# Three tiles' memberships as one stationary operand, a staged prologue, and the output written inside the loop of a graph-attention kernel

## Chip, core and metric

One NeuronCore of one Trainium2 chip runs the kernel; `num_devices=1`. The time is device microseconds (us) of one launch, the median of three runs. TensorE (PE, its weight loads PEld), VectorE (DVE), ScalarE (ACT), GpSimd (POOL) and SyncE (SP) each run their own instructions in order and wait for each other through semaphores. SP, ACT and POOL also issue DMAs.

## The reference, cut to what matters

A graph of 12,500 nodes and 412,500 edges, sorted by destination `dst`, is passed once through a four-head attention layer:

```python
h = jnp.maximum(_layernorm(x, axis=-1), 0.0)            # 12500 x 128
h = (h @ W_node.T).reshape(num_nodes, H, HD)            # H = 4, HD = 32
e = (edge_features @ W_edge.T).reshape(num_edges, H, HD)
att = jnp.sum(jnp.concatenate([h[src], h[tgt], e], -1) * a, -1)
att = jnp.where(att > 0, att, 0.2 * att)
m = jnp.maximum(segment_max(att, tgt), 0.0)
ex = jnp.exp(att - m[tgt])
denom = segment_sum(ex, tgt) + (num_edges - deg)[:, None] * jnp.exp(-m)
out = x + segment_sum((ex / denom[tgt])[:, :, None] * h[src], tgt)
```

So every edge needs one row of its source node, and rows are then summed over runs of edges with equal destination.

## The kernel before

**Prologue.** 12,500 nodes are 98 blocks of 128 (`NB`). Line 276 goes over groups of seven blocks: load `x` (SP), layer norm statistics (DVE, L289, L290), square root (ACT, L292), normalise and ReLU (ACT, L302), transpose (PE, L304; copied out by DVE, L306), project with the weights (PE, L309), copy out (ACT, L310), and store the group into a DRAM table of 140-float rows (`table`, L314, issued by ACT). A row holds the node's attention terms and its 128 projected values with a 1 after each head. Before this loop the kernel looks through the destinations: lowest destination and smallest step of each chunk of 896 edges (L207 to L217), from these the chunk's 32-wide window of nodes and several small rows (L224 to L262), and, for all edges at once, `key`, an edge's place in its chunk's window (L265 to L274, most of it on POOL). The whole prologue is ordered by a planner, not by the order of the code.

**Main loop.** A chunk is 7 tiles of 128 edges, a batch 8 chunks, and there are 461 chunks in 58 batches. This part is in `tc.manual_schedule()` (L560): each engine gets its instructions in the order of the code. For batch `b`:

* `gather` (L357): POOL issues one indirect DMA per tile (L364), which fetches 128 table rows into `hs`; 56 per batch, for batch `b+1` while batch `b` is worked on. Three small POOL copies, the gates (L360), stand ahead of the gathers of parts 0, 1 and 2 (18, 19 and 19 gathers, `STOPS`). A gate reads a result of earlier work, and so holds POOL until that work is done. Gate 0 reads the sums of batch `b-1` (`merged`), gate 1 the sums of the first two chunks of batch `b` (`s.pas`), gate 2 those of chunks 4 and 5.
* `weigh` (L398): when the 56 tiles of batch `b` have landed, DVE transposes the attention terms (`zst`, L402), and DVE and ACT find a running maximum per destination and the exponentials (`exr`).
* `scatter` (L429): for each chunk ACT and DVE make `rhs` (7 tiles x 140 columns; L442, L444), and PE multiplies it, tile by tile, with `hot`, the 128 x 32 membership of the tile's edges in the window (L449). Tile `i` goes to the 32 PE columns numbered `i % 4`. ACT copies the sums of two chunks out of PSUM (`keep`, L458).
* `begin` (L373): DVE makes `mem` (L377) and `hot` (L393), PE the attention terms `z` of batch `b+1` (L382, L385).
* `collect` (L462) adds the four column groups up on PE; every second batch `merge` (L475) rescales and scans 16 chunks on DVE (among it the two products of L514) and adds them to `acc` (L523), the sums of all nodes, in SBUF.
* After batch 3, `count_windows` (L525) counts chunks that do not fit one window.

**Rest.** `window()` (L621) handles those chunks in a loop on a count read from the chip. For these inputs the count is zero: the widest chunk spans 30 nodes. Then lines 802 to 833 turn `acc` into the output: weights, PE moves the heads back to rows, `x` is added, stores.

Of the kernel before, what the change touches and what calls it, by code (L numbers as in the profile page):

```python
# [11 lines left out]
I32 = mybir.dt.int32  # L12
# [22 lines left out]
COLS = NSC * CT  # L35
HALF = 4 * P
# [5 lines left out]
GB = 7  # L42
FH = 2 * H
# [12 lines left out]
def tiles_of(sc):  # L56

    return [T if c < NCH - 1 else max(LAST, 4) for c in (2 * sc, 2 * sc + 1) if c < NCH]


def filled(sc):

    return [T if c < NCH - 1 else LAST for c in (2 * sc, 2 * sc + 1) if c < NCH]

# [10 lines left out]
def kernel(  # L75
# [32 lines left out]
    key = const.tile([P, COLS], BF16, name="key")  # L108
    acc = const.tile([P, NQ, AW], F32, name="acc")
    nc.gpsimd.memset(acc, 0.0)  # L110
# [38 lines left out]
    def index(b):  # L149
        t = indices.tile([P, SB * CT], I32, name="src")  # L150
        nc.sync.dma_start(t, src[:, b * SB * CT:(b + 1) * SB * CT])
        return t

    early = [index(b) for b in range(2)]


    with (
        tc.tile_pool(name="prep1", bufs=1) as p1,
# [10 lines left out]
        dsts = p1.tile([P, COLS], I32, name="dsts")  # L169
        nc.scalar.dma_start(dsts, dst)  # L170
# [35 lines left out]
        for g in range(NG):  # L206
            n = min(P, NC2 - g * P)  # L207
            dch = p2.tile([P, CE], I32, name="dch")
            nc.sync.dma_start(dch[:n, :], dstc[g * P:g * P + n, :])
            nc.vector.tensor_reduce(ext[:n, g, 0:1], dch[:n, :], AX.X, OP.min)  # L210
            rise = p2.tile([P, CE - 1], I32, name="rise")
            nc.gpsimd.tensor_tensor(rise[:n, :], dch[:n, 1:], dch[:n, :CE - 1], op=OP.subtract)
            nc.vector.tensor_reduce(ext[:n, g, 1:2], rise[:n, :], AX.X, OP.min)
            pen = p2.tile([P, CE + 1], F32, name="pen")
            nc.gpsimd.memset(pen, -BIG)
            nc.vector.tensor_scalar(pen[:n, 1:CE], rise[:n, :], 0.0, -BIG, op0=OP.not_equal, op1=OP.mult)
            nc.sync.dma_start(pens[g * P:g * P + n, :], pen[:n, :])  # L217
        pb = [pps.tile([P, NC2], F32, name=f"pb{k}", bufs=1) for k in range(2)]
# [14 lines left out]

        floor = p1.tile([P, NC2], F32, name="floor")
# [24 lines left out]
        for a in range(4):  # L259
# [5 lines left out]
        dl = p1.tile([P, COLS], I32, name="dl")  # L265
        nc.vector.tensor_scalar(dl, dsts, W - 1, None, op0=OP.bitwise_and)
        rel = p1.tile([P, COLS], F32, name="rel")
        nc.gpsimd.tensor_copy(rel, dsts)
        nc.gpsimd.tensor_tensor(rel.rearrange("p (c t) -> p c t", t=T), rel.rearrange("p (c t) -> p c t", t=T),
                                floor[:, :, None].to_broadcast([P, NC2, T]), op=OP.subtract)  # L270
        nc.gpsimd.tensor_scalar(rel, rel, float(W), float(W), op0=OP.is_ge, op1=OP.mult)
        low_f = p1.tile([P, COLS], F32, name="dsts")
        nc.gpsimd.tensor_copy(low_f, dl)
        nc.gpsimd.tensor_tensor(key, rel, low_f, op=OP.add)  # L274

        for b0 in range(0, NB, GB):
            xg = p2.tile([P, GB, D], F32, name="xg")
            n = min(GB, -(-(N - b0 * P) // P))
            full = min(n, (N - b0 * P) // P)
            nc.sync.dma_start(xg[:, :full, :],  # L280
                              x[b0 * P:(b0 + full) * P, :].rearrange("(b p) d -> p b d", p=P))
            if full < n:
                nc.vector.memset(xg[:, full, :], 0.0)
                rest = N - (b0 + full) * P
                nc.sync.dma_start(xg[:rest, full, :], x[(b0 + full) * P:N, :])
            mv = p2.tile([P, GB, 2], F32, name="mv")
            for i in range(GB):
                stats = p2.tile([P, 6], F32, name="stats")
                nc.vector.bn_stats(stats, xg[:, i, :])  # L289
                nc.vector.bn_aggr(mv[:, i, :], stats)  # L290
# [138 lines left out]
    def scatter(s, follow):  # L429

        out = []
        for j in range(SB):
            sc = s.b * SB + j
            tiles = tiles_of(sc)
            if not tiles:
                continue
# [432 lines left out]
```

## Time and profile before

| what | us |
|---|---|
| median of three runs | 4327.94 (4326.93 to 4329.52) |
| profiled execution, its own time | 4340.74 |
| its span, first to last instruction | 4339.0 |
| start to first gather | 183.4 |
| first gather to end of the last | 4064.6 |
| end of the last gather to the end | 91.0 |
| POOL, DVE, PE, ACT busy | 3162.1, 1756.9, 1260.8, 453.5 |

The three stretches add up to the span. Busy time of an engine counts its instructions, not the time in which it waits or issues; a gather's issue between two gathers is therefore idle time of POOL in the page. PEclk is the share of TensorE's full clock that was granted, and was 0.595 on average.

### The profile page before, as it was taken

The page shows a single profiled execution, that of the slowest core. Times are in us where ns is not written, and L with a number is a line of the kernel's source. Part 1 is how long each engine was busy: PE and PEld are TensorE (multiplying, and loading weights), DVE is VectorE, ACT ScalarE, POOL GpSimd, SP SyncE. Part 2 cuts the span into 40 slices and gives each one's busy share as a digit, 9 for nine tenths or more (in the row PEclk, how much of TensorE's full clock was granted, in tenths as well). Part 3 has the DMA queues.
Part 4 walks back from the last instruction along what each step waited for, and adds up shares of the span by engine and source line. Part 5 has one row for each costly group of instructions (what it writes and reads, how often), then busy time and mean ns, then how long its engine had stood idle before and what let it go on. Part 6 is the DMA issues. An engine that isn't in the chain of part 4 may idle for free. (4 is left out here: it accounts for less than half of the span.)

```text
span 4339.0 us, 30729 instructions
## 1 busy us (share of the span) xinstructions
PE 1260.8 (29%) x9107; PEld 535.4 (12%) x9107; DVE 1756.9 (40%) x3136; ACT 453.5 (10%) x1430; POOL 3162.1 (73%) x3422
## 2 busy tenths in 40 slices
PE   3613131313232222313131323232232313131324
PEld 2301010101011110101010101111010101010101
DVE  7325343444334342534343433434253434343346
ACT  2301010100101010101010000101010101010010
POOL 5277777777777777777777777777777777777771
PEclk8556565656555655556565656565655656565655
DMA  3433433333343334343343434343434333343434
GB/s 96 139 91 94 112 106 93 105 91 109 86 110 85 109 86 109 86 108 103 93 106 89 110 87 110 85 110 86 109 85 109 96 99 104 90 108 88 109 86 129
DMA packets 235471, 434.48 MB, mean 100 GB/s; under 512 B 85642, under 2 KB 135814, under 8 KB 235174
## 3 DMA queue, kind: packets, MB, share of 16 engines
q0 software_dynamic: 103136, 231.23, 23.5%
q1 hardware_dynamic: 118678, 192.44, 13.5%
q10 hardware_dynamic: 13488, 8.82, 0.6%
q8 instruction: 73, 1.20, 0.1%
q14 instruction: 96, 0.79, 0.1%
HBM read 417.15 MB, written 15.09 MB: 100 GB/s over the span
## 5 line engine op out<-in xcount | busy, mean ns | idle before, releaser
L364 POOL DMA_INDIRECT hs<-table,src x3223 | 3072.6, 953 | 1067.5 <-issue 1043.4
L449 PE MATMUL pa<-rhs,hot 128*32 128x140 f32 x6448 | 516.8, 430 | 2900.8 <-DVE rhs L444 2888.2
L402 DVE STREAM_TRANSPOSE zst<-hs 128x224 f32<-128x224 f32 x58 | 23.9, 412 | 1867.0 <-DMA hs<-table,src 1867.0
L449 PEld LDWEIGHTS pa<-rhs,hot 128*32 128x32 f32 x6448 | 271.4, 152 | 3148.3 <-issue 2740.1
L444 DVE TENSOR_TENSOR rhs<-hs,exr 128x924 f32<-128x924 f32 x461 | 515.0, 1117 | 151.2 <-ACT rhs L442 151.2
L382 PE MATMUL z<-eft,wa 128*32 128x384 f32 (+1 forms) x928 | 433.2, 627 | 16.2 <-DMA twb<-table 16.2
L411 ACT ACTIVATE a<-z 32x224 f32<-32x224 f32 x232 | 80.5, 347 | 2057.6 <-DVE z L410 2057.6
L385 PE MATMUL z<-mem,twb 128*32 128x512 f32 x464 | 186.7, 546 | 3.9 <-DMA twb<-table 3.9
L382 PEld LDWEIGHTS z<-eft,wa 128*32 128x32 f32 x928 | 119.1, 128 | 305.9 <-issue 300.1
L442 ACT COPY rhs<-exr 128x28 f32<-128x28 f32 x461 | 97.9, 212 | 332.3 <-DVE rhs L444 276.9
L420 ACT ACTIVATE both<-a 32x224 f32<-32x224 f32 x232 | 89.9, 388 | 376.3 <-DVE a L417 372.0
L393 DVE TENSOR_TENSOR hot<-exr,key 128x448 f32<-128x448 f32 x231 | 127.5, 611 | 0.0
L523 DVE TENSOR_TENSOR acc<-acc,a 128x70 f32 x461 | 109.7, 238 | 34.3 <-DVE acc L523 19.6
L458 ACT COPY m<-pa 128x280 f32<-128x280 f32 x231 | 90.5, 392 | 310.9 <-PE pa L449 310.9
L410 DVE TENSOR_TENSOR z<-z,zst 32x224 f32<-32x224 f32 x232 | 89.8, 387 | 77.9 <-ACT a L411 71.9
L416 DVE TENSOR_TENSOR_SCAN m<-pen,up 32x896 f32<-32x896 f32 x58 | 116.4, 2008 | 7.8 <-DVE up L414 0.5
L414 DVE TENSOR_TENSOR_SCAN up<-pen,z 32x896 f32<-32x896 f32 x58 | 117.0, 2017 | 2.0
L485 DVE TENSOR_SCALAR mc<-r 128x16 f32<-128x16 f32 (+1 forms) x29 | 5.6, 192 | 249.1 <-ACT r L473 249.1
L377 DVE TENSOR_SCALAR mem<-mem,nid 128x896 f32<-128x896 int32 x116 | 81.2, 740 | 26.3 <-DMA mem<-in_dstc 26.3
L422 DVE SCALAR_TENSOR_TENSOR both<-pen,m 32x224 f32<-32x224 f32 x232 | 88.7, 382 | 2.4
L473 ACT COPY r<-t 128x280 f32<-128x280 f32 (+1 forms) x58 | 23.7, 409 | 592.3 <-PE z L385 591.4
L467 PE MATMUL t<-m,rsame 128*32 128x280 f32 (+1 forms) x464 | 73.4, 415 | 0.4 <-ACT m L458 0.4
(142 smaller groups left out, 994.9 us busy)
## 6 DMA issues: line engine op xcount, KB each, us to landing
eft<-in_ef SPq DMA_DIRECT2D x58, 1792.0 KB
mem<-in_dstc SPq DMA_DIRECT2D x116, 448.0 KB
hs<-table,src POOLq DMA_INDIRECT x3223
xg<-in_x SPq DMA_DIRECT2D x26, 448.0 KB
twb<-table SPq DMA_DIRECT2D x464, 0.5 KB
table<-rows ACTq DMA_DIRECT2D x14, 490.0 KB
pen<-pens SPq DMA_DIRECT2D x58, 112.1 KB
out<-o SPq DMA_DIRECT2D x13, 448.0 KB
```

Of the source, the lines that this page charges most:

```text
L364: nc.gpsimd.indirect_dma_start(out=s.hs[:, i, :], out_offset=None, in_=table[:, :], in_offset=bass.IndirectOffsetOnAxis(ap=s.src[:, i:i + ...
L382: nc.tensor.matmul(s.z[:, part], wa3[:, j, :], s.eft[:, j, part], start=(j == 0), stop=False)
L385: nc.tensor.matmul(s.z[:, part], twb[:, s.b % 2, k, :], s.mem[:, k, part], start=False, stop=(k == 1))
L393: nc.vector.tensor_tensor(hot, rows_ps[:, None, :].to_broadcast([P, CT, W]), key[:, sc * CT:(sc + 1) * CT, None].to_broadcast([P, CT, W]), ...
L414: nc.vector.tensor_tensor_scan(up, s.pen[:, :CE], s.z, 0.0, op0=OP.add, op1=OP.max)
L416: nc.vector.tensor_tensor_scan(m[:, ::-1], s.pen[:, CE:0:-1], up[:, ::-1], 0.0, op0=OP.add, op1=OP.max)
L420: nc.scalar.activation(both[g * R:(g + 1) * R, 0, :, :], grouped(att, g), AF.Exp)
L442: nc.scalar.copy(rhs[:, :n, :, HD + 2], s.mx[:, :n, q * H:(q + 1) * H])
L444: nc.vector.tensor_tensor(rhs[:, :n, :, :HB], s.hs[:, i0:i0 + n, FH:].rearrange("p t (h d) -> p t h d", h=H), s.ex[:, :n, q * H:(q + 1) * ...
L449: nc.tensor.matmul(pa[g * W:(g + 1) * W, c, :], s.hot[j][:, c * T + i, :], rhs[:, i, :, :].rearrange("p h k -> p (h k)"), start=(i < 4), s ...
L458: nc.scalar.copy(s.pas[:, 2 * j:2 * j + n, :], pa[:, :n, :])
L523: nc.vector.tensor_tensor(cols, cols, put[:, i0 + i, :, :], op=OP.add)
```

## The change

1. **`scatter`.** Three tiles' memberships stand side by side as one stationary operand of 96 columns, and three tiles' `rhs` as one moving operand of 420 columns. The result is 96 x 420, of which only the three 32 x 140 blocks on the diagonal mean anything. Seven tiles take three matmuls (tiles 0-2, tile 6 alone, tiles 3-5) instead of seven. `keep` is called for each chunk and copies the three blocks with three ACT copies; gate 1 reads the block sums of chunk 1 on 96 partitions. `collect` adds three groups.
2. **Prologue.** It is in manual order. Units of three blocks go through stages that are written out one after another (`measure`, `deviate`, `normalize`, `project`, `turn`, `keep_rows`), each unit a few rounds behind the next; `x` is loaded in groups of nine blocks, three loads ahead. The look through the destinations is spread over the rounds (`extents`), its loads go out on ACT's queue, and the chain of small rows stands after the last round. The clearing of `acc` comes after POOL's first two instructions on the destinations.
3. **`key`** is no longer made for all edges in the prologue, but per batch in `begin`, by four DVE operations on 128 x 56.
4. **`merge`** copies its 128 x 32 `lastm` part to PSUM (`here`) and multiplies from there.
5. **Output in the loop.** `parts()` says after which batch a run of blocks can no longer change. `finish` makes its output there, seven blocks at a time, in 15 parts; its store is issued in the next batch. `count_windows` also checks that this was allowed for the given input, and if not (or if there are windows) the loop at the end computes all output once more. For these inputs the check gives zero and the loop is not entered.

```diff
@@ tiles_of ... @@
+def parts():
+    got, b0 = [], 0
+    for n in [GB] * 13 + [3, NB - 13 * GB - 3]:
+        last = (b0 + n) * P + 2 * W
+        b = next((b for b in range(MB - 1, NBT, MB) if (b + 1) * CB * CE * N >= last * E), NBT - 1)
+        got.append((b0, n, b if b0 + n < NB else NBT - 1))
+        b0 += n
+    return got
@@ prologue @@
+        def extent(g):
+            rise = p2.tile([P, CE - 1], I32, name="rise", bufs=NG)
+            nc.gpsimd.tensor_tensor(rise[:n, :], dch[:n, 1:], dch[:n, :CE - 1], op=OP.subtract)
...
+            nc.vector.tensor_reduce(ext[:n, g, 0:1], dch[:n, :], AX.X, OP.min)
+            yield
+            nc.vector.tensor_reduce(ext[:n, g, 1:2], rise[:n, :], AX.X, OP.min)
+            yield
+            nc.vector.tensor_scalar(pen[:n, 1:CE], rise[:n, :], 0.0, -BIG, op0=OP.not_equal, op1=OP.mult)
+            nc.sync.dma_start(pens[g * P:g * P + n, :], pen[:n, :])
+            yield
...
+        while k < 0 or line:
+            u = next(units, None)
+            if u:
+                measure(u)
+            at = {j: v for j, v in line}
+            if k + 3 in at:
+                deviate(at[k + 3])
+            if k + 2 in at:
+                normalize(at[k + 2])
+            if k in at:
+                project(at[k])
+            if k + 2 in at:
+                turn(at[k + 2])
+            if k in at:
+                keep_rows(at[k])
...
+            if k > 6 and k % 2:
+                next(extents, None)
+            k += 1
+        for _ in extents:
+            pass
         pb = [pps.tile([P, NC2], F32, name=f"pb{k}", bufs=1) for k in range(2)]
...
-        nc.gpsimd.tensor_scalar(rel, rel, float(W), float(W), op0=OP.is_ge, op1=OP.mult)
-        low_f = p1.tile([P, COLS], F32, name="dsts")
-        nc.gpsimd.tensor_copy(low_f, dl)
-        nc.gpsimd.tensor_tensor(key, rel, low_f, op=OP.add)
@@ begin @@
+        nc.vector.tensor_scalar(dk, s.dst, W - 1, None, op0=OP.bitwise_and)
+        nc.vector.tensor_tensor(key.rearrange("p (c t) -> p c t", t=T), s.dst.rearrange("p (c t) -> p c t", t=T),
+                                floor[:, s.b * CB:(s.b + 1) * CB, None].to_broadcast([P, CB, T]), op=OP.subtract)
+        nc.vector.tensor_scalar(key, key, float(W), float(W), op0=OP.is_ge, op1=OP.mult)
+        nc.vector.tensor_tensor(key, key, dk, op=OP.add)
@@ scatter @@
-                for i in range(n):
-                    g = i % 4
-                    nc.tensor.matmul(pa[g * W:(g + 1) * W, c, :], s.hot[j][:, c * T + i, :],
-                                     rhs[:, i, :, :].rearrange("p h k -> p (h k)"),
-                                     start=(i < 4), stop=(i + 4 >= n), tile_position=(0, g * W))
-                if c == 0 and len(out) > 1:
-                    keep(s, *out[-2])
-                    follow(out[-2][0])
+                pa = ps.tile([P, G * H * AW], F32, name="pa", bufs=2)
+                order = [*range(0, n - G, G), n - G] if n % G == 0 else [0, n - n % G, *range(G, n - n % G, G)]
+                for i in order:
+                    w = min(G, n - i)
+                    nc.tensor.matmul(pa[:w * W, :w * H * AW],
+                                     s.hot[j][:, c * T + i:c * T + i + w, :].rearrange("p t r -> p (t r)"),
+                                     rhs[:, i:i + w, :, :].rearrange("p t h k -> p (t h k)"),
+                                     start=(i == order[0]), stop=(i == order[-1]))
+                if last is not None:
+                    keep(s, *last)
+                    if last[0] % 2:
+                        follow(last[0] // 2)
+                last = (q, pa)
+    def keep(s, q, pa):
+        for g in range(G):
+            rows = slice(g * W, (g + 1) * W)
+            nc.scalar.copy(s.pas[rows, q, :], pa[rows, g * H * AW:(g + 1) * H * AW])
@@ merge @@
-        here = lastm[:, c0:c0 + n, :]
+        here = ps.tile([P, MC, 2], F32, name="t2")[:, :n, :]
+        nc.vector.tensor_copy(here, lastm[:, c0:c0 + n, :])
@@ finish, new @@
+        nc.sync.dma_start(xg[:, :full, :], x[b0 * P:(b0 + full) * P, :].rearrange("(b p) d -> p b d", p=P))
...
+        nc.scalar.activation(em, acc[:, q, AW - 1], AF.Exp, scale=-1.0)
...
+        nc.vector.tensor_tensor(wgt[:, :n * 4, :], acc[:, q, :HD], em[:, :, None].to_broadcast([P, n * 4, HD]),
+                                op=OP.mult)
...
+        for h in range(H):
+            for s in range(4):
+                nc.tensor.matmul(po[s * W:(s + 1) * W, h // 2, h % 2, :n, :],
+                                 ident[:, h * W:(h + 1) * W], w4[:, :n, s, :], start=True, stop=True,
+                                 tile_position=(0, s * W))
+        for k in range(2):
+            cols = xg[:, :n, k * 2 * HD:(k + 1) * 2 * HD].rearrange("p b (h d) -> p h b d", d=HD)
+            nc.vector.tensor_tensor(cols, po[:, k, :, :n, :], cols, op=OP.add)
@@ main loop @@
+                for store in stores:
+                    store()
...
+            for b0, n, last in parts():
+                if last == b:
+                    stores.append(finish(work, ps, "up", em_ps, b0, n))
```

## The prediction, made before the changed kernel had run

> **What bounds the kernel now.** I read the page's costliest groups first, then the timeline at the start, through one late batch and at the end, and last the windows view for the granted clock.
>
> ```profile
> L364 POOL DMA_INDIRECT hs<-table,src x3223 | 3072.6, 953 | 1067.5 <-issue 1043.4
> ...
> L402 DVE STREAM_TRANSPOSE zst<-hs 128x224 f32<-128x224 f32 x58 | 23.9, 412 | 1867.0 <-DMA hs<-table,src 1867.0
> ```
>
> POOL's gathers are the bound: 953 ns busy and some 0.30 us of issue each. Their start-to-start interval is 1.252 us in the median; 3222 of these are 4034 us of the 4064.6 us between first and last gather. DVE meanwhile stands idle for 1867 us until a batch has landed. Only three things can move the end: when the first gather starts, what stretches gathers or holds a gate, and what follows the last one.
>
> ```profile
> 53.99 11.51 POOL L271 TENSOR_SCALAR rel<-rel 128x3248 f32<-128x3248 f32 x1
> 54.39 11.18 DVE L261 TENSOR_SCALAR nid<-top,rcol 32x116 f32<-32x116 f32 x1
> ...
> 183.43 1.18 POOL L364 DMA_INDIRECT hs<-table,src  x1 [110.43 <-issue]
> ```
>
> The start: until 76 us little of the node loop is done; POOL makes `key`, and a DVE instruction that elsewhere takes 0.31 us takes 11.18 beside it. Then eleven groups at 7.9 us each follow.
>
> ```profile
> 4209.10 0.20 POOL L360 COPY gate<-r 128x1 f32<-128x1 f32 x1
> ...
> 4210.85 0.41 DVE L402 STREAM_TRANSPOSE zst<-hs 128x224 f32<-128x224 f32 x1 [18.94 <-DMA hs<-table,src]
> ...
> 4223.86 1.12 DVE L444 TENSOR_TENSOR rhs<-hs,exr 128x924 f32<-128x924 f32 x1 [0.27 <-ACT rhs L442]
> ...
> 4225.13 1.15 PE L449 MATMUL pa<-rhs,hot 128*32 128x140 f32 x14 [49.03 <-DVE rhs L444]
> ...
> 4227.70 0.39 ACT L458 COPY m<-pa 128x280 f32<-128x280 f32 x1 [1.08 <-PE pa L449]
> ...
> 4231.70 0.19 POOL L360 COPY gate<-m 128x1 f32<-128x1 f32 x1
> ```
>
> One batch, with the end of its last gather as zero (4209.10): PE starts at 16.05, the first `keep` ends at 19.0, gate 1 runs at 22.6. So gate 1 has 3.6 us to spare; over all batches after the first it is 3.54 in the mean, and 0.13 in the batch after `count_windows`. This margin is what the change draws on.
>
> **The change part by part.**
>
> **(a) Prologue.** A unit is three blocks. DVE: statistics and their aggregation now wait for each other, one block 0.41 us (95.42 to 95.72 is one such wait, plus 0.11), three 1.23; reciprocal and shift 0.41, `hT` copy 0.53, ones and `tn` 0.2: 2.37. ACT: square root 0.30, three ReLUs 1.26 (row at 95.11), row copy 0.45: 2.0, and every third unit a DMA issue of 0.38 that waits for DVE's ones; I charge 0.19 per unit. PE at half clock: six projection passes 1.73 (76.54), three transposes 0.9: 2.63. Three engines nearly tie; I take 2.6. The destination steps add two reductions of 1.08 and one 0.62 for each of four groups, 9.5 within the rounds. First `x` at 7 us[...], POOL blocking DVE early 2, two short rounds 3, 31 x 2.6 = 80.6, 9.5, the last rounds 6: 108. Then the chain of small rows: in the built program the first gather waits for its last `nid`. The same instructions undisturbed are 12.6 us by their rows (`top` 1.12, fourteen of 0.62 to 0.64 or 0.38 to 0.46, `nid` 4 x 0.31), before them 2 for the last reduction and eight matmuls, after them 1 to POOL's start. Sum 124; with some rounds at the warm clock I take 122. Saved: 183.4 - 122 = **61**. Bounds: units of 2.37 give 115, units of 3.0 give 135: saved 48 to 70. The table's last store (landed 4 us after its issue) is covered by that chain.
>
> **(b) `key`.** Removed with (a). Four DVE operations per batch, 0.54 us together, lie in DVE's idle time. `mem` (L377), 1.4 us of a similar kind, stretched gathers by 0.1 us per batch; 0.54 us gives **+2**, bounds 0 to 8.
>
> **(c) `here` in PSUM.**
>
> ```profile
> 4180.80 2.12 DVE L514 TENSOR_TENSOR a<-up,lastm 128x544 f32<-128x544 f32 x2
> 4181.54 1.14 POOL L364 DMA_INDIRECT hs<-table,src  x1 [0.30 <-issue]
> ```
>
> Of the gathers that overlap L514, 26 are longer than 1.25 us, by 10.4 us in sum. L444, as long but with one operand in PSUM, stretches the gathers beside it hardly (114 intervals, 1.4 us in the gathers' own durations). The extra copy is 0.2 us per merge in DVE's idle time. **-9.5**, bounds -11 to -6.
>
> **(d) `scatter` and gate 1.** A chunk was 14 PE passes of 140 columns (each product is recorded as two) in four column groups that overlap: 1.15 us. Now it is four passes of 420 and two of 140, all through the same columns: 1960 streamed columns.
>
> ```profile
> 4237.90 0.18 PEld L382 LDWEIGHTS z<-eft,wa 128*32 128x32 f32 x1 [0.68 <-issue]
> 4238.75 0.18 PEld L382 LDWEIGHTS z<-eft,wa 128*32 128x32 f32 x1 [0.68 <-issue]
> ```
>
> ```profile
> 4225.00:4228.40 3.40, 2.79 (x38) 1.73 (x41) 2.40 (x3) 0.93 (x4) 2.49 (x4) 0.50 0.26 63
> ...
> 4236.00:4240.00 4.00, 4.00 (x11) 0.95 (x6) 2.15 (x4) 0.39 (x1) 3.08 (x4) 0.56 0.26 57
> 4240.00:4247.00 7.00, 7.00 (x27) 2.24 (x26) 0.00 (x0) 0.00 (x0) 5.26 (x6) 1.00 0.27 60
> ```
>
> The first two rows: passes of 512 columns stand 0.853 us apart at clock 0.50, so 1.67 ns a column, with their weight loads hidden. A chunk is then 3.27 us, two chunks 6.54. The Trainium skill (TensorE: Matmul & The Clock Gate, Part 3, Packing small matmuls) speaks against this edit: narrow outputs should be packed into distinct column groups, where it saw three run 2.38 times as fast. By its factor, spread over the old passes, the old chunk would be 14 x 0.233 / 2.38 = 1.37 us; the row has 1.15, which I use. Either way PE triples its time.
>
> The windows rows (PE's busy time first, PEclk third from the end) show the clock: 0.50 while PE was 82% busy in `scatter`, 1.00 only after a full stretch of `z`. The same page's Part 1 says that the clock doubles after one busy window of about 3.4 us that runs free of the program. By it, `scatter`, now without gaps, turns warm 3 to 6.3 us after its start, and two chunks take 4.8 to 6.4 us, 5.6 in the middle; by the old `scatter`'s row, 6.54. I follow the page, since `z` did turn warm within 4 us. So: 16.05 + 5.6, drain 0.15, three ACT copies (0.28 for a 140-column copy alone, 0.19 each behind another: 0.66), semaphores 0.1: 22.6, with ends 21.8 and 23.5. Gate 1 is due at 22.6. Spread evenly, the late part is 0.29 us in the mean, over 57 batches **+17**; bounds 0 and 57 x 0.95 = +54. Behind the gate stand 19 gathers, and behind these everything. Gates 0 and 2 have over 15 us. ACT's `rhs` copies now queue behind `keep`, which slows later chunks to some 2.3 us; the scatter ends about 7 us later, and DVE still had 18.9 us idle before `zst` in this merge batch.
>
> **(e) `count_windows`**, once: its batch had 0.13 us at gate 1; the later scatter and its 14 small fills make it late by about 7: **+7**, bounds 2 to 12.
>
> **(f) Output in the loop.** Removed at the end: from the last `acc` add (4281.9) to 4339. A part costs about 5 us of DVE and PE (weights 1.08, adds 4 x 0.32, PE 1.1 to 1.9, reciprocal 0.2, the rest small), 13 or 14 times, within the 18.9 us of idle DVE less 8 for (b) to (d). Without that cover it would be 70. Its loads and stores (448 KB, two per part on SP) come into a stage whose DMA share is 0.38; SP's next loads are due a batch later. **+1.5** for stretched gathers, bounds 0 to 10. After the last gather: PE's start 16.1; five chunks 5.6, then 2.3, 2.3, 1.4 give 27.7; `keep` and `collect` 1.7; the merge as before (4271.44 to 4281.87) and `here`, 10.6: 40. The last part is small (four blocks): exponential to adds 3.8, store issue 0.4, landing 2, leaving 1: 47. Before 91.0. **-44**, bounds -47 to -38.
>
> **Sum:** -61 + 2 - 9.5 + 17 + 7 + 1.5 - 44 = -87. The span 4339.0 becomes 4252. The profiled execution (4340.74) ran 12.8 above the median of the runs; taking 87 off that median gives **4241**.
>
> **The rivals.**
>
> *Gate 1 never feels the warm clock.* For: in the old `scatter` it mostly stayed at 0.50 until `z`. Against: PE had gaps then. +54 instead of +17: 4278.
>
> *Gate 1 holds nothing.* ACT's copies and the clock come out better and the prologue's units are 2.37: -17 and -7: 4217.
>
> *Slower: weight loads no longer hide.* The old products used four column groups; now each load goes to columns that are streaming. A 128-column load's record is 0.18 us at half clock, six per chunk, two chunks: +2.2 us on gate 1 at a cold clock, 3.1 late, 57 x 3.1 = 177 against 17: 4401. It turns the sign once gate 1 is late by (87 + 17) / 57 = 1.8 us per batch. Against it: `z` has all its loads in the same columns and stands exactly at its stream time.
>
> *It doesn't shorten the prologue*, since waits between stages add up to 3.4 us per unit: 4241 + 25 = 4266.
>
> **How the numbers follow.** Likeliest case 0.5 (4241, own range 4205 to 4265), cold gate 0.2, no hold 0.13, long prologue 0.07, slower 0.08, other 0.02. The range takes in the likeliest, the cold gate with the other upper bounds, and the no-hold case: 4198 to 4312. Within 0.2% (8.7 us, about what a measurement here can tell) 0.02; slower 0.09; faster 0.89.
>
> **What would show it.** First gather near 122 us; gathers beside L610 at 0.95; `pa` in three products, two chunks in 5 to 6.5 us, and the gate's row with a wait on ACT; after the last gather 47 us. Wrong if the first gather is after 140, if gate 1 waits over 1 us per batch, or if `zst` no longer waits for the DMA.

## The result, and the profile after

The changed kernel takes 4299.31 us (median of 4 runs, 4298.43 to 4300.09); the kernel before took 4328.73 us beside it. The ratio is 0.9932, interval 0.9914 to 0.9949: 29 us faster, where 87 were forecast. The time lies in the range that was given, far above its likeliest value.

The profiled execution took 4299.55 us, its span 4297.8. The span of before, 4339.0, was taken at a slightly slower pace of the gathers: their median interval was 1.252 us there and is 1.249 here, and 3222 x 0.003 = 9.7 us of the difference are that pace, not the change. This would also explain most of the 12.8 us by which the profiled execution of before stood above its median.

Costliest groups of the kernel after (busy us, mean ns of one, idle us before them and what ended most of it):

```profile
L447 POOL DMA_INDIRECT hs<-table,src x3223 | 3052.6, 947 | 1060.8 <-issue 1058.0
L539 PE MATMUL pa<-rhs,hot 128*96 128x420 f32 (+1 forms) x2762 | 1092.5, 519 | 2216.8 <-DVE rhs L531 2216.3
...
L493 DVE STREAM_TRANSPOSE zst<-hs 128x224 f32<-128x224 f32 x58 | 23.9, 411 | 1356.2 <-DMA hs<-table,src 1356.2
L553 ACT COPY m<-pa 32x140 f32<-32x140 f32 x1383 | 367.3, 266 | 762.8 <-PE pa L539 752.1
```

POOL's gathers are still the bound, and `zst` still waits for the last of them, so DVE kept cover (1356 us of it instead of 1867). New is what POOL itself waited for (us in total, times, longest):

```profile
POOL gate L443 <- ACT m L553: 63.4, 56, 5.5
```

Gate 1 holds in all 57 batches that have one (the trace puts a 57th wait, of 1.4 us, down to ACT's `rhs`). One batch in the timeline, to be read against the one shown of before:

```profile
2050.05 0.20 POOL L443 COPY gate<-r 128x1 f32<-128x1 f32 x1
...
2051.72 0.41 DVE L493 STREAM_TRANSPOSE zst<-hs 128x224 f32<-128x224 f32 x1 [8.59 <-DMA hs<-table,src]
...
2065.96 8.69 PE L539 MATMUL pa<-rhs,hot 128*96 128x420 f32 x18 [24.05 <-DVE rhs L531]
...
2067.57 0.18 PEld L539 LDWEIGHTS pa<-rhs,hot 128*32 128x32 f32 x2 [1.25 <-issue]
...
2072.75 0.82 ACT L553 COPY m<-pa 32x140 f32<-32x140 f32 x3 [1.71 <-PE pa L539]
...
2073.70 0.18 POOL L443 COPY gate<-m 96x1 f32<-96x1 f32 x1 [1.09 <-ACT m L553]
...
2074.38 0.97 POOL L447 DMA_INDIRECT hs<-table,src  x1 [0.51 <-issue]
```

With the end of the last gather (2050.05) as zero: PE starts at 15.9, the three copies of chunk 1 end at 23.5, the gate runs at 23.65 after a wait of 1.09, and the next gather needs 0.51 us of issue where it otherwise needs 0.30. Before, the gate ran at 22.6 and had 3.5 us to spare.

The start and the end of the kernel after:

```profile
62.03 0.48 ACT L315 COPY rows<-ph 128x420 f32<-128x420 f32 x1
...
65.16 0.49 ACT L315 COPY rows<-ph 128x420 f32<-128x420 f32 x1
...
67.22 0.51 ACT L315 COPY rows<-ph 128x420 f32<-128x420 f32 x1
...
110.53 1.29 DVE L395 TENSOR_SCALAR nid<-top,rcol 32x116 f32<-32x116 f32 x4
...
112.85 1.15 POOL L447 DMA_INDIRECT hs<-table,src  x1 [82.67 <-issue]
...
4245.94 0.39 DVE L501 TENSOR_TENSOR z<-z,zst 32x224 f32<-32x224 f32 x1 [2.83 <-PE z L468]
...
4260.15 8.92 PE L539 MATMUL pa<-rhs,hot 128*96 128x420 f32 x18 [13.78 <-DVE rhs L531]
...
4284.72 0.20 ACT L670 ACTIVATE exr<-acc 128x16 f32<-128x16 f32 x1 [8.74 <-DVE acc L619]
...
4289.78 1.24 SPq L694 DMA_DIRECT2D out<-xg  x1
```

The first gather starts at 112.85 (before 183.43), the last ends at 4240.88, and 56.9 us follow (before 90.9). So where the time went, span against span, with the intervals of the gathers sorted by their place in the batch:

| | forecast, us | measured, us |
|---|---|---|
| first gather (a) | -61 | -70.6 |
| gaps at gate 1 (d, e) | +24 | +82.3 |
| gaps at gates 0 and 2 | 0 | -0.8 |
| all other gaps, at equal pace (b, c, f in the loop) | -6 | -8.4 |
| after the last gather (f) | -44 | -34.0 |
| sum | -87 | -31.5 |

"Gaps" is the sum over all batches of start-to-start intervals less 1.252 us: 85.7 at gate 1's place after, 3.4 before. -31.5 and the pace of -9.7 make the -41.2 between the spans. One row carries the error: gate 1.

### The profile page after: what moved, and what is told of

It reads as the page before. It is cut to its first block, busy times and chain, and to the rows that moved or that the text cites. A ratio compares the mean times of both kernels' runs of the same rounds, so it can differ in the third digit from the quotient of the medians.

```text
span 4297.8 us, 25217 instructions
## 1 busy us (share of the span) xinstructions
PE 1767.8 (41%) x5421; PEld 572.8 (13%) x5421; DVE 1788.9 (42%) x3449; ACT 746.4 (17%) x2606; POOL 3107.8 (72%) x3417
## 3 DMA queue, kind: packets, MB, share of 16 engines
q0 software_dynamic: 103136, 231.23, 20.9%
## 4 chain that ended last, share of the span: by engine, by line
POOL 45%; issue 18%; DVE 14%; PE 9%; ACT 6%; DMA 5%; DVEq 0%; POOLq 0%; ACTq 0%
POOL hs L447 44%; PE pa L539 9%; DMA hs<-table,src 5%; DVE up L505 3%; DVE m L507 3%; ACT both L511 2%; DVE z L501 2%; ACT a L502 2%; DVE rhs L531 2%; DVE z L503 1%; DVE a L508 1%; DVE exr L517 1%; ACT m L553 1%; DVE zst L493 1%; POOL gate L443 0%
## 5 line engine op out<-in xcount | busy, mean ns | idle before, releaser
L539 PE MATMUL pa<-rhs,hot 128*96 128x420 f32 (+1 forms) x2762 | 1092.5, 519 | 2216.8 <-DVE rhs L531 2216.3
L539 PEld LDWEIGHTS pa<-rhs,hot 128*96 128x96 f32 (+1 forms) x2762 | 333.3, 159 | 2968.6 <-issue 2693.8
L553 ACT COPY m<-pa 32x140 f32<-32x140 f32 x1383 | 367.3, 266 | 762.8 <-PE pa L539 752.1
L465 PE MATMUL z<-eft,wa 128*32 128x384 f32 (+1 forms) x928 | 361.6, 543 | 23.3 <-DMA twb<-table 23.3
L465 PEld LDWEIGHTS z<-eft,wa 128*32 128x32 f32 x928 | 97.7, 110 | 283.0 <-issue 283.0
L684 PE MATMUL up<-a,ident 128*32 128x224 f32 (+2 forms) x480 | 45.2, 555 | 214.8 <-DVE a L677 214.8
L460 DVE TENSOR_SCALAR mem<-mem,nid 128x896 f32<-128x896 int32 x116 | 74.7, 685 | 21.9 <-issue 16.2
```

The lines of the kernel that those rows point to most:

```text
L465: nc.tensor.matmul(s.z[:, part], wa3[:, j, :], s.eft[:, j, part], start=(j == 0), stop=False)
L539: nc.tensor.matmul(pa[:w * W, :w * H * AW], s.hot[j][:, c * T + i:c * T + i + w, :].rearrange("p t r -> p (t r)"), rhs[:, i:i + w, :, :].r ...
L553: nc.scalar.copy(s.pas[rows, q, :], pa[rows, g * H * AW:(g + 1) * H * AW])
```

## The experiments

All are the kernel after with one edit, except where said. Ratios are to the kernel before on the same chip; the kernel after has 0.9932.

**1. Is it the scatter that holds gate 1?** Two ways: put the old `scatter`, `keep`, `collect` and gate back, or leave all as it is and let the gates stand four gathers later.

```diff
-                    nc.tensor.matmul(pa[:w * W, :w * H * AW], ...
+                    nc.tensor.matmul(pa[g * W:(g + 1) * W, c, :], s.hot[j][:, c * T + i, :],
+                                     rhs[:, i, :, :].rearrange("p h k -> p (h k)"),
+                                     start=(i < 4), stop=(i + 4 >= n), tile_position=(0, g * W))
...
-                        gather(batch(b + 1), 1 + j // 2, s.pas[:G * W, 2 * j + 1, 0:1])
+                        gather(batch(b + 1), 1 + j // 2, s.pas[:, 2 * j, 0:1])
```

> The kernel after with the scatter, keep, collect and gate read of before: 14 products of 32 x 140 in four column groups and one eviction per pair of chunks (part d alone undone; key, here in PSUM, output in the loop and the new prologue stay). Theory 1 (the growth of the loop is gate 1 waiting for the longer scatter): the wait at gate 1 falls from 63 us to about 0 to 5, gaps at the gate-1 position lose some 80 us, the loop from first to last gather is about 4045 us, and the tail falls by about 9 us with the shorter scatter: span about 4208, median about 4210. Rival (the loop grew because the added key, output parts and their DMAs stretch gathers or hold the gate): the loop stays at 4128 and the time stays at about 4290 to 4299. Rival 2 (the gate stands for something that will wait anyway elsewhere): less than 40 us gained.

```diff
-STOPS = (0, 18, 37)
+STOPS = (0, 22, 41)
```

> The kernel after with gates 1 and 2 standing four gathers later in the row (before gathers 22 and 41 instead of 18 and 37), nothing else. Gate 1 becomes due about 5 us later (4 x 1.25), some 27.6 us after the last gather, and its release comes at 23.6. Theory 1: it then holds nothing outside the batch after the window count (0 to 1 us there), the gap at that position loses 80 to 85 us, the tail stays at 57: about 4215 us. Rival (the wait moves to gate 2 or to the wait of zst): 4260 to 4299. The period of a batch falls from 71.65 to about 70.2 us and the starts of the scatter no longer stand at one phase of the clock's 3.413 us windows.

Measured: the old scatter 4220.14 us against 4337.84, ratio 0.973 (0.9713 to 0.9746); the later gates 4233.45, ratio 0.976 (0.9744 to 0.9776). What the gate waited for, old scatter first:

```profile
POOL gate L443 <- ACT rhs L533: 0.8, 1, 0.8
```

```profile
POOL gate L443 <- ACT m L553: 4.2, 1, 4.2
```

The gaps at gate 1 fell from 85.7 to 4.0 and 0.1 us, the loop from 4128.0 to 4057.6 and 4063.4 us, though both runs had the slower pace of 1.252 us, which accounts for the 10 us by which the old scatter missed its forecast of 4210. With the later gates the median batch takes 70.48 us. Only the one wait behind `count_windows` is left with the later gates. Both rivals fall: the key, the output parts and their DMAs don't carry the loss, and the wait doesn't come back elsewhere in full. A little does: gate 1's new place holds 7.4 us of gaps, 4.2 of them that one wait, and the loop is 5.8 us longer than with the old scatter. The old scatter also takes 8.5 us off the end (tail 48.4), as expected; the later gates leave it (57.6).

Then both gates were taken out, with the new scatter and with the old one. (The gates are no part of the result; gate 0 still keeps a batch's gathers behind the batch that read the same buffer.)

```diff
-STOPS = (0, 18, 37)
+STOPS = (0,)
...
-                    if b + 1 < NBT and j in (0, 2):
-                        gather(batch(b + 1), 1 + j // 2, s.pas[:G * W, 2 * j + 1, 0:1])
+                    pass
```

> The kernel after without gates 1 and 2: a batch's 56 gathers follow gate 0 in one row, nothing else is changed. Theory (the gates' only effect on the time is their wait and their own small cost): against the later gates (ratio 0.976 to before) it also loses the two gate copies and what stands around them, about 0.2 us a batch, 12 us: ratio about 0.973. Rival (without the gates the gathers run into something that the gates kept them from, a full queue or a buffer not free): the wait comes back at a gather or at gate 0, ratio 0.98 to 0.99.

> The kernel after with the scatter of before and without gates 1 and 2: a version meant to beat both kernels. From the run with the old scatter (ratio 0.973): its two gate positions and the ones behind them hold some 12 us above the median interval; without them the ratio is about 0.970. Rival: the gates cost nothing on the path, 0.973.

Measured: 4218.30 us, 0.9733 (0.9718 to 0.9748), and 4208.30 us, 0.971 (0.9696 to 0.9725), both against 4333.48. As expected, to 0.001. The last is the fastest version that was run: some 2.2% below the kernel after and 2.9% below the one before.

**2. Why did a chunk take longer than its streamed columns?** In the trace of after, chunk 0 takes 3.73 us at half clock, where 1960 columns at 1.67 ns make 3.27. The third product has a 32 wide stationary operand, the others 96. Taken with the 96 wide slice of its three tiles and written to the third diagonal block, it streams the same columns and never changes the width.

```diff
                     w = min(G, n - i)
-                    nc.tensor.matmul(pa[:w * W, :w * H * AW],
-                                     s.hot[j][:, c * T + i:c * T + i + w, :].rearrange("p t r -> p (t r)"),
+                    f = i if i == 0 or w == G else i + w - G
+                    nc.tensor.matmul(pa[:G * W, (i - f) * H * AW:(i - f + w) * H * AW],
+                                     s.hot[j][:, c * T + f:c * T + f + G, :].rearrange("p t r -> p (t r)"),
```

> The kernel after with the third product of a chunk (the single tile) taken with the same 96 wide stationary slice of its three tiles and written to the third diagonal block's columns: the same 140 streamed columns and the same kept result, but no change of the stationary operand's width inside a chunk. Theory 1 (the 0.46 us of a chunk above its stream time are weight loads that stand exposed where the width changes): chunk 0 takes 3.27 to 3.35 us instead of 3.73, and PE is through both chunks some 0.5 us earlier at the same clock phase. Rival (the exposure belongs to the start of a new accumulation or to new data, not to the width): chunk 0 stays at 3.7. For the time: linear theory 57 x 0.5 = -28, about 4270 us; lock theory: the scatter's start moves to about 0.3 us into the window, the period stays at 71.65 and the time at 4299, unless that phase lies too near the window's edge, and then the lock breaks and the time falls by 30 to 60 us.

Measured: chunk 0 of one batch, first in the kernel after, then in this run (both rows end 0.2 us behind the start of the next chunk, for they hold the modelled end of the last pass):

```profile
2065.96 3.94 PE L539 MATMUL pa<-rhs,hot 128*96 128x420 f32 x6 [24.05 <-DVE rhs L531]
```

```profile
2269.65 3.55 PE L540 MATMUL pa<-rhs,hot 128*96 128x420 f32 x6 [42.85 <-DVE rhs L531]
```

From start to start chunk 0 takes 3.34 us in nearly every batch (3.05 where the clock turned warm inside it), so 0.39 us of each cold chunk belonged to the change of width; the rival falls. The starts of the single passes in after say where: beyond its streamed columns a pass takes 0.13 us more ahead of the narrow product, 0.14 more behind it and 0.11 one pass later. The 0.08 us at the chunk's first pass stay with one width. The time is 4278.31 us against 4337.84, ratio 0.9864 (0.9848 to 0.9881), some 29 us below the kernel after. By time alone that is the plain sum of what was saved, the linear theory of the expectation. The scatter's starts tell more, and come next.

**3. Why is gate 1 late by nearly the same amount in every batch?** The forecast spread the warm clock's arrival evenly over 3 to 6.3 us after the scatter's start, as if the program and the clock's windows ran free of each other. (Every change of the granted clock in the trace falls on a grid of 3.413 us; a window is one step of it.) Three successive starts of PE's scatter in the kernel after:

```profile
2137.70 1.69 PE L539 MATMUL pa<-rhs,hot 128*96 128x420 f32 x2 [41.77 <-DVE rhs L531]
2209.29 1.69 PE L539 MATMUL pa<-rhs,hot 128*96 128x420 f32 x2 [41.65 <-DVE rhs L531]
2280.99 1.69 PE L539 MATMUL pa<-rhs,hot 128*96 128x420 f32 x2 [41.72 <-DVE rhs L531]
```

They are 71.59 and 71.70 us apart; the median over the run is 71.65, and 21 windows are 71.68. Put on the grid, most of the starts stand 1.05 to 1.4 us into a window, and after a disturbance they go back in steps (2.96, 2.13, 1.67, 1.47, 1.35, 1.27 us in six batches), while in the kernel before they are spread over the whole window. My second theory was that the batch period, from one start to the next, has locked to the clock: a scatter that starts later in its window meets the warm clock sooner after its start, and so is done less late; each microsecond of delay costs half a microsecond less at the gate, until 56 gathers and the wait make just 21 windows. Its rival is the plain sum.

The half can be read from the batches themselves. Behind that disturbance the starts stand 1.75, 0.92, 0.46, 0.26, 0.14 and 0.06 us beyond 1.21, about where they settle: each batch roughly halves the distance. The periods from these starts are 70.84, 71.22, 71.48, 71.56 and 71.61 us, shorter the later the start. A straight line through period against start (without the first six batches and those that a disturbance stretched) falls by 0.48 us for each us in after. It falls by 0.47 to 0.49 in the run with one width and in the next three below, taken over starts beyond 0.75 us; in the kernel before, where gate 1 has slack, it rises by 0.07. The two theories part further where a little is added or taken away.

```diff
             nc.scalar.copy(s.pas[rows, q, :], pa[rows, g * H * AW:(g + 1) * H * AW])
+            if q == 1 and g == 0:
+                nc.scalar.copy(s.pas[rows, q, :], pa[rows, 0:H * AW])
```

> The kernel after with one more copy of the first kept block of chunk 1, behind the same copy on ACT: about 0.27 us more before gate 1 in every batch, nothing else. Lock theory (the batch period has locked to 21 of the clock's windows, 71.68 us, because a later start of the scatter meets the warm clock earlier): the period stays at 71.65 us, the phase of the scatter's start moves by about twice the delay, from about 1.2 to about 1.75 us into the window, and the time stays within 8 us of 4299. Linear theory (what is added before gate 1 is added to the batch): 57 x 0.27 = +15, about 4315 us, period 71.92.

Measured: 4308.68 us against 4337.84, ratio 0.9932 (0.9916 to 0.9949), the same as without the added copy; the plain sum asked for 0.9968. The ratio alone proves little, since the pace of this run (1.252) lengthens the kernel before as well. Its starts:

```profile
2144.25 1.69 PE L539 MATMUL pa<-rhs,hot 128*96 128x420 f32 x2 [41.84 <-DVE rhs L531]
2215.86 1.69 PE L539 MATMUL pa<-rhs,hot 128*96 128x420 f32 x2 [41.77 <-DVE rhs L531]
2287.68 1.68 PE L539 MATMUL pa<-rhs,hot 128*96 128x420 f32 x2 [41.94 <-DVE rhs L531]
```

The median period is 71.69 us, and the starts have moved to about 2.2 us in the window. That is 1.0 us later than in after, not 0.55: this run's gathers had the slower pace (1.252), which adds 0.17 us to a batch, and the copy cost 0.30; twice their sum is 0.94. The 11th and the 49th start, in after and in this run:

```profile
919.12 0.98 PE L539 MATMUL pa<-rhs,hot 128*96 128x420 f32 x1 [24.06 <-DVE rhs L531]
...
3642.91 0.98 PE L539 MATMUL pa<-rhs,hot 128*96 128x420 f32 x1 [41.65 <-DVE rhs L531]
```

```profile
925.76 0.99 PE L539 MATMUL pa<-rhs,hot 128*96 128x420 f32 x1 [24.17 <-DVE rhs L531]
...
3649.59 0.98 PE L539 MATMUL pa<-rhs,hot 128*96 128x420 f32 x1 [41.85 <-DVE rhs L531]
```

The 38 batches between them take 2723.79 and 2723.83 us; 38 times 21 windows are 2723.84. By the plain sum pace and copy would have added 38 x 0.47 = 18 us. What was added came back as an earlier warm clock. The 9.4 us by which this run is longer than after (4308.68 for 4299.31) lie where the starts had not settled: 5.9 us in the first ten batches, while they move from 0.56 to 2.2 us in the window, and 3.2 in the last nine, which hold a disturbance.

The other side: the gate waits for fewer of the three kept blocks, so that it comes 0.27 or 0.54 us earlier.

```diff
-                        gather(batch(b + 1), 1 + j // 2, s.pas[:G * W, 2 * j + 1, 0:1])
+                        gather(batch(b + 1), 1 + j // 2, s.pas[:2 * W, 2 * j + 1, 0:1])
```

(and `s.pas[:W, ...]` for the second).

> The kernel after, with gate 1 (and 2) waiting for the first two of the three kept blocks only, 0.27 us less before the gate. Lock theory: the scatter's start about 0.55 us earlier in the window than in the kernel after at the same pace of gathers (1.05 at 1.252 us, 0.65 at 1.249), period 71.65 to 71.7, ratio 0.993. Linear theory: 57 x 0.27 = -15 us, ratio 0.9897.

> The kernel after, with gate 1 (and 2) waiting for the first kept block alone, 0.54 us less before the gate. Linear theory: 57 x 0.54 = -31 us, ratio 0.986. Lock theory: start 1.1 us earlier than in the kernel after: at 1.252 us a gather about 0.5, still inside, ratio 0.993; at 1.249 about 0.1, past the edge between 0.28 and 0.44, so that the lock breaks now and then and the ratio is 0.98 to 0.986.

Measured: 0.27 us less gives 4301.66 us against 4324.50, ratio 0.9947 (0.9933 to 0.9960), no gain; period 71.69. But this doesn't separate the theories: the gaps at gate 1 fell by 13.5 us, about what the plain sum says, and the intervals of one place in the batch, the 27th, grew by 16.2 (from 4.7 to 20.9). The 27th gather runs beside DVE's two `mem` products in `begin`; in after, and then in this run:

```profile
2298.97 1.28 DVE L460 TENSOR_SCALAR mem<-mem,nid 128x896 f32<-128x896 int32 x2
2299.43 1.05 POOL L447 DMA_INDIRECT hs<-table,src  x1 [0.30 <-issue]
```

```profile
2300.98 1.27 DVE L460 TENSOR_SCALAR mem<-mem,nid 128x896 f32<-128x896 int32 x2
2301.13 1.35 POOL L447 DMA_INDIRECT hs<-table,src  x1 [0.30 <-issue]
```

How long this gather takes goes with where it starts against the first product. In the median it starts 0.46 us behind it in after and takes 1.03 us; here 0.16 behind and 1.34; in the next run 0.11 ahead and 0.94, as most gathers do. So what the gate saved was spent again eight gathers later. The batch's own work did not change, and the starts stood at 1.33 us, not at the 0.65 expected.

0.54 us less gives 4265.03, ratio 0.9865 (0.9849 to 0.9880), which both theories allow. Its starts are no longer 71.68 apart:

```profile
2120.17 1.68 PE L539 MATMUL pa<-rhs,hot 128*96 128x420 f32 x2 [41.17 <-DVE rhs L531]
2191.43 1.69 PE L539 MATMUL pa<-rhs,hot 128*96 128x420 f32 x2 [41.14 <-DVE rhs L531]
2262.88 1.68 PE L539 MATMUL pa<-rhs,hot 128*96 128x420 f32 x2 [41.13 <-DVE rhs L531]
```

In the window they run 1.37, 1.45, 0.79, 0.43, 0.14 and then jump to 2.62, over and over: they slide towards the window's start, and where a scatter begins within 0.30 us of it (0.31 is already too late) the clock turns warm a whole window sooner, 3.1 us after the start instead of 6.5, the gate is early, and the next start jumps. The same saw-tooth shows in the run with one width, with its edge between 0.67 and 0.70 us. So the lock has an edge, and what a saving is worth depends on whether it reaches it.

A long delay, six copies instead of one:

> The kernel after with six more copies of the first kept block of chunk 1 on ACT: about 1.75 us more before gate 1 in every batch. Linear theory: 57 x 1.75 = +100 us against after (ratio to before about 1.016). Lock theory: a start one window length later gains at most 1.7 us, so no phase gives 21 windows any more; the starts move on by 0.5 to 2.2 us from batch to batch, most slowly at the window's edges, about 1.16 us in the mean: 57 x 1.16 = +66 us against after, ratio to before about 1.0085, and the phases are spread over the window again.

Measured: 4401.29 us against 4333.48, ratio 1.0159 (1.0143 to 1.0175): the linear theory's number, some 98 us more than after by the ratios, for 57 x 1.75 = 100, and my +66 is refuted. I had taken the edge at 0.7 us from the run with one width, where the scatter of after has it at about 0.3 (in this run 0.19 was early enough and 0.28 was not). The starts are not spread either: they alternate between about 0.5 and 2.65 us, and the periods between 73.8 and 72.9, which is 43 windows for two batches (146.8 us). So the time speaks for the sum, the phases for a lock to another ratio, and the time alone can't tell them apart here.

**4. Part (c) alone**, in the kernel before:

```diff
-        here = lastm[:, c0:c0 + n, :]
+        here = ps.tile([P, MC, 2], F32, name="t2")[:, :n, :]
+        nc.vector.tensor_copy(here, lastm[:, c0:c0 + n, :])
```

> The kernel before with one part of the change: in merge, the pairs of masks are copied to PSUM first and the products read them there (part c alone). Theory (the two long products slow the gathers beside them while both their operands lie in SBUF): the gathers beside them return to 0.95 us, loop and time -9.5 us (bounds -11 to -6), ratio 0.9978. Rival (the slowing is that of the output's or of any long DVE instruction): 0 us, ratio 1.000.

Measured: 4330.27 us against 4333.48, ratio 0.9991 (0.9982 to 1.0000), so -4 us within -8 and 0. In the trace the intervals at the four places where the products of `merge` lay lost 10.7 us (12.3 to 1.6), while some other places, at or just behind the gates, gained: all gaps together fell by 6.3 us at the run's own pace (1.251). The effect is there with the expected size, and part of it is given back.

**5. Runs on another chip.** The shorter gates were first run, beside the kernel after, on a chip where the kernel before took 5070 us.

> The kernel after once more, beside the two runs with a shorter gate, so that phases and intervals can be compared at the same pace of the gathers. Lock theory: at a median gather interval of 1.252 us (56 of them 0.17 us longer than at 1.249) the scatter's start stands at about 1.6 us in the window instead of 1.2, and the period is 71.65 to 71.7 us all the same; ratio 0.993. Linear theory: the period is longer by the gathers' 0.17 us, 71.82.

> The kernel after, with gate 1 (and 2) waiting for the first two of the three kept blocks of its chunk only: some 0.27 us less before the gate in every batch, nothing else. Lock theory: the scatter's start moves earlier in the window by about 0.55 us (to about 1.05 at the slow pace of gathers, 0.65 at the fast one), the warm clock comes that much later after it, the period stays at 71.65 to 71.7 and the ratio at 0.993. Linear theory: 57 x 0.27 = -15 us, ratio 0.9897.

> The kernel after, with gate 1 (and 2) waiting for the first kept block alone: 0.54 us less before the gate. Linear theory: 57 x 0.54 = -31 us, ratio 0.986. Lock theory: the phase would have to be 1.1 us earlier than in the kernel after. At the slow pace of gathers that is about 0.5 and still inside (the run with the long delay turned warm late down to 0.44): period and ratio unchanged, 0.993. At the fast pace it is about 0.1, past the edge: the window counts as busy from its start, the warm clock comes a window earlier, the lock breaks now and then, and the ratio is about 0.98.

> The kernel after once more, as the measure for the two runs with a shorter gate on the same chip. Ratio 0.993. Lock theory: the scatter's start at about 1.2 us in the window at a median gather interval of 1.249 us, 1.6 at 1.252, the period 71.65 to 71.7 either way.

> The kernel after, with gate 1 (and 2) waiting for the first two of the three kept blocks only, 0.27 us less before the gate. Lock theory: the start about 0.55 us earlier in the window than in the kernel after beside it (1.05 at the slow pace, 0.65 at the fast one), period 71.65 to 71.7, ratio 0.993 as there. Linear theory: 57 x 0.27 = -15 us, ratio 0.9897.

> The kernel after, with gate 1 (and 2) waiting for the first kept block alone, 0.54 us less before the gate. Linear theory: 57 x 0.54 = -31 us, ratio 0.986. Lock theory: start 1.1 us earlier than in the kernel after: at the slow pace about 0.5, still inside, ratio 0.993; at the fast pace about 0.1, past the edge between 0.28 and 0.44, so that the lock breaks now and then and the ratio is 0.98 to 0.986.

Measured, in two sets: the kernel after 5422.31 and 5416.27 us (1.0688 and 1.0686), 0.27 us less 5398.34 and 5402.76 (1.0649 and 1.0664), 0.54 us less 5347.42 and 5339.02 (1.0541 and 1.0537). The gathers had their usual length. The second run of the kernel after, ACT in one scatter, then what PE did meanwhile:

```profile
2121.74 0.21 ACT L529 COPY rhs<-exr 128x28 f32<-128x28 f32 x1
2136.30 0.82 ACT L553 COPY m<-pa 32x140 f32<-32x140 f32 x3 [14.35 <-issue]
2137.15 0.21 ACT L529 COPY rhs<-exr 128x28 f32<-128x28 f32 x1
2151.71 0.82 ACT L553 COPY m<-pa 32x140 f32<-32x140 f32 x3 [14.35 <-remote]
```

```profile
2121.12 4.28 PE L539 MATMUL pa<-rhs,hot 128*96 128x420 f32 x12 [0.29 <-issue]
2138.65 3.93 PE L539 MATMUL pa<-rhs,hot 128*96 128x420 f32 x6 [13.26 <-issue]
```

Two pauses of 14 us stand in this scatter. ACT is the engine that stands: PE had made the sums that it copies at 2136.30 by 2125.40, while DVE waits for ACT's next `rhs`, and PE for DVE. The trace names nothing of the program that ended them. Of the 47 waits of 13 to 15 us on ACT in the run 43 lie in every second batch. Here they stand between gates 1 and 2; over the run the gaps at gate 1 are 694 us and at gates 0 and 2 517. They swamp the phases, so these six runs say nothing on the lock. They do say that the change's sign isn't the same everywhere: there it made the kernel 6.9% slower, and the two kernels with a shorter gate lost a little less. Why this chip pauses, and why the change suffers more, stays open.

## Why the prediction was wrong where it was

**(d), the step that failed.** "Gate 1 is due at 22.6. Spread evenly, the late part is 0.29 us in the mean, over 57 batches +17; bounds 0 and 57 x 0.95 = +54." The mechanism was named rightly (longer scatter, gate 1, a wait on ACT) and the size was not: 1.13 us of wait in the mean and 0.2 us of slower restart behind it. (The forecast's own ends of 21.8 and 23.5 make the mean 0.24 us and the most 0.9; that slip is 3 us.) A gate that waits over 1 us per batch is also one of the signs of being wrong that the prediction named. Four terms were short:

- The chunks: 3.73 us each at half clock instead of 3.27, since the weight loads of `z`, which I took as the pattern, all have one width. Halved by the warm clock: 0.46 us at the end of chunk 1. The rival "weight loads no longer hide" had the right mechanism at 2.2 us for two chunks; it is 0.46 us per chunk, and experiment 2 shows that 0.39 of it sits at the change of width. (Its 0.18 us for a 128-column load are those of the full clock: the rows of L304 at 23 to 26 us in before, where the granted clock is 1.00. At half clock such a load takes 0.34 us there, L309, and a 96-column one 0.285 in after.)
- The clock: warm at about 5.6 us in nearly every batch, not evenly from 3 to 6.3. From the mean of 4.65, half of the difference is 0.45 us. The rule that I followed holds: the clock turns warm at the end of the first window that the scatter fills, but for at most its first 0.3 us. In these two rows of one scatter, PE's busy time stands first and the granted clock third from the end. That the arrival is spread evenly was my addition.

```profile
2065.90:2071.50 5.60, 5.54 (x10) 1.73 (x10) 1.54 (x2) 1.16 (x5) 4.24 (x5) 0.50 0.54 142
2071.50:2078.00 6.50, 6.05 (x19) 1.94 (x18) 2.93 (x3) 2.71 (x11) 3.98 (x5) 0.99 0.18 44
```

- ACT's three copies: 0.82 us, not 0.66. The 0.19 for a copy behind another was too low; each is 0.27.
- The semaphore, 0.13 for 0.1, and the restart of the gathers, 0.2, which was left out.

0.46 + 0.45 + 0.16 + 0.03 + 0.20 is 1.30 us on a gate that would have been due just then; 57 x 1.30 = 74 of the 82. The upper bound of +54 failed because it bounded only the clock and held every other term fixed. With the lock, though, the lateness isn't such a sum: the batch waits out what is missing to 21 windows (71.68 less the 70.3 that 56 gathers and the gates' own cost take, 1.38), as long as the terms together fall inside its reach. The added copy of experiment 3 shows this on one side. On the other side only the edge was seen, for the one saving that stayed inside it was spent again at the 27th gather.

**(a)** -70.6 for -61, just past the bound of -70. Row copies of three blocks follow each other in 2.06 us in the median, where I took 2.6 (the copies at 65.16 and 67.22 are such a pair; the step from 62.03 holds a reduction of the destinations). I had charged PE at half clock; it was granted 0.66 to 1.00 in the windows of this stage. The chain behind the rounds took 13 us as forecast, and the last `nid` is right ahead of the first gather.

**(c)**, **(b)** and the loop's part of **(f)**: -8.4 for -6, as forecast; (c) alone in the kernel before came out smaller in time than in its gathers. With the old scatter in place the added `key` and output parts leave the other gaps at 11.4 us, against 10.8 for (c) alone in the kernel before, at a pace 1 ns faster: they cost next to nothing.

**(e)** The batch after `count_windows` waited 5.5 us at gate 1, some 4 more than the others; +7 was forecast.

**(f), the tail**: -34 for -44, 56.9 us for 47. By its steps: PE starts 19.3 us after the last gather, not 16.1, because `z` of the last batch is itself late (the row at 4245.94: 2.83 us of wait for PE, whose `z` follows the longer scatter); five chunks, `keep` and merge 24.5 for 24; the last part 6.3 for 4.2, its 32 small products alone 1.93 and the issue of the second store 1.24; and 6.8 us from the last store's issue to the end, where I allowed 3. That the old scatter's tail is 48.4 shows 8.5 of the 56.9 to be the scatter's length; my step had counted the scatter in front of the end but not the one in front of `z`.

**The rivals.** "Gate 1 never feels the warm clock" was nearest in time (4278) but wrong in kind: the clock does come, too late and always at the same point. The prologue did shorten. The bound didn't change engines. The sign was right because (a) and (f) together were worth 105 us; had gate 1 been late by 0.5 us more in each batch, the change would have made nothing.

## What to carry to other kernels

When work on a chain with 3.5 us of slack is made longer, sum every link between the start of the work and the release (streamed columns, loads where the operand's shape changes, each eviction, the semaphore, the restart of what waited), and bound the links together, not one at a time. A release point is cheaper to move than the work in front of it: two numbers in `STOPS`, or no gate at all, gave back nearly all that the new scatter had cost in the loop. And where a wait of a periodic program ends at an event of the clock, look whether the period has settled on the clock's grid: then a small addition may cost nothing, as 38 batches with the added copy show. That a small saving buys nothing until it breaks the lock follows from the same slope, but no run here shows it by itself.

## What the hardware did that was not expected

- A batch of some 70.3 us of own work ran at 71.65 to 71.69 us, 21 of the clock's 3.413 us windows, at two paces of the gathers and with 0.30 us added to it, and a start off its place came back by half in each batch; with 1.75 us added it ran at 43 windows for two batches.
- Two changes of the stationary operand's width, 96 to 32 and back, cost an fp32 chunk 0.39 us at half clock (3.73 us for 3.34 with one width), with both widths loaded from the same tile.
- A gather beside DVE's `mem` product took 0.94 to 1.35 us, by where it started: 0.94 with a start 0.11 us ahead of the product, 1.34 with one 0.16 us behind it, 1.03 at 0.46.
- The gathers' pace itself differs between executions: 1.249 to 1.252 us in the median, 10 us over the kernel.
